# Two expert blocks as planned steps at the end of pass 1, and the weights of three relations made in a branch

## Chip, core and metric

The kernel runs on one core of one Trainium2 chip. TensorE (PE) multiplies matrices, VectorE (DVE), ScalarE (ACT) and GpSimd (POOL) work on rows, SyncE (SP) issues most transfers. All data begin and end in the chip's memory. The metric is the device time of one launch in microseconds: 2520.09, the median of three runs (2518.72 to 2521.66). The profile is one further execution, which took 2517.28 us; the span that its records cover is 2515.3 us.

## The reference

The input x is 64 x 256 rows (16,384 tokens) of 256 numbers, in fp32; adj is 64 x 256 x 256 integers, here 0 or 1. Two layers, each a graph step and a feed-forward step, all with a residual:

```python
x = x + gnn0(layernorm(x), adj)      # masked softmax attention over the neighbours
x = x + mamba2(layernorm(x))         # one chunk of 256, 8 heads, conv of 4, gate, RMS norm, W_out, W_lin
x = x + gnn1(layernorm(x), adj)      # sum over 4 relations r of (adj == r) @ x @ weight[r], + bias
x = x + moe(layernorm(x))            # below

logits = x @ gate_w + gate_b                          # 8 experts
idx, prb = argmax(softmax(logits)), max(softmax(logits))
pos = (rank of the token among those of its expert, in order of tokens)
kept = pos < 2560                                     # 1.25 * 16384 / 8
hmid = relu(buf[idx, pos] @ w1[idx] + b1[idx])        # 256 -> 1024
y = (hmid @ w2[idx] + b2[idx]) * prb * kept           # 1024 -> 256
x + nan_to_num(y, nan=0, posinf=1e4, neginf=-1e4)
```

Relation r counts the neighbours whose adj equals r, so with adj of 0 and 1 only the first relation contributes.

## The kernel before, in words

**Preparation** (L420 to L505). Weights are centred, so that the layer norms need no mean, and extended by columns that give the routing logits and row sums directly. Helpers work on one matrix at a time, with matmuls on TensorE and copies on VectorE, through a pool of two PSUM buffers: `centred` subtracts column means (L396), `projected` transposes a matrix, multiplies it by the gate weights and copies the result. The four relations' weights are loaded, centred and projected one after the other into `every`; the first is copied to `wrel` in on-chip memory, all four are stored to `wreld` in the chip's memory. Then follow the biases (L454), the attention vectors, W_out times W_lin, and b1, turned and stored (`b1d`).

**Pass 1** (L587 to L1163) takes 32 groups of two batch items, 512 tokens each, through both graph steps, the mamba step and the routing logits: `attention`, `scan`, `mix`, `relate`. `relate` makes hr = xhi, xlo times the adjacency (part of L585, where all products of the plan are recorded), multiplies it by `wrel`, adds the bias `brel` by an accumulating transfer into the tile x, adds the product (L1047), and issues two stores of x on SP, to `x3d` (a copy in the chip's memory from which pass 2 gathers) and to `out`. After each second group `choose` routes 1,024 tokens: some 25 small operations, a running count per expert (`seen`, L1103), two matmuls that turn counts into positions, and eight indirect scatters of (token, probability, row sum, row scale) into `slots`, an array of 2,560 places for each expert (L1123).

**The order of pass 1** is a plan. Every operation is a `Step` with an engine, an estimated duration and the tiles that it reads and writes; `Plan.record` builds all engines' streams by a list simulation. At each turn it takes, for each engine, the ready step that can begin earliest, and among those within 0.05 us the lowest rank, which is `PACE * g + DUE[k]` for step k of group g. Tiles are reused by tag, PSUM is eight banks given out by the simulation. Only these streams reach the chip, where engines wait for each other by semaphores; the simulated times do not.

**Between the passes.** `list_blocks` counts tokens per expert and makes the list of blocks for pass 2 on VectorE, in plain program order behind the plan. A test (`general`) sends adjacency values other than 0 and 1 to a branch (`again > 0`) that does pass 1 over with all four relations, read from `wreld`, through `AtOnce`, an executor that emits each step where it is written. With the inputs used here the branch is not taken.

**Pass 2** (L1195 to L1349) runs the experts over blocks of their places: wholes of 512 and halves of 256 rows, up to 40 and 8, each behind an `If` on the counts. A block loads its rows of `slots` (L1222) and its expert's w1, b1, w2, b2 (2 MB) on SP, gathers rows of `x3d` on POOL (L1251), scales them (L1260), transposes them (L1272), computes 8 hidden products with a relu on ScalarE (L1298, L1302) and, for each 128 rows, an output product of 8 matmuls (L1308), bias and scale (L1313, L1314), the guard against non-finite numbers, the residual (L1319 to L1328), and an indirect scatter to `out` (L1329). Loads and gathers of the next blocks are issued one or two blocks ahead; the first ones wait for pass 1's end.

Of the kernel before, what the change touches and what calls it, by code (L numbers as in the profile page):

```python
# [30 lines left out]
PACE = 21.50  # L31
DUE = [
    -273, -768, -7, 206, -128, -104, -233, 716, 257, 96, 325, 660, -290, -837, -1156, -195, -739,
    -864, 633, -563, -1270, 205, -488, -744, -1044, 252, -389, 419, -601, -43, 36, 132, 68, -155,
    389, 355, -223, -943, 4, 450, -281, 40, -502, 21, 982, 124, 113, 525, -49, 159, 104, 239, 309,
    -615, -359, -749, 426, 428, -391, -391, -326, -1237, -329, -546, -645, -815, -544, -187, -763,
    -683, -372, -601, -139, 290, -500, 172, -270, -586, 121, -388, 994, 458, -317, 125, 17, 277,
    17, 326, -210, -907, 100, -221, -383, -517, 6, 127, 610, 247, -329, -914, -875, -432, -1394,
    67, -309, 571, -93, -248, 110, 916, -78, 172, 34, 14, -122, 417, 67, 66, -569, 10, -1389, 19,
    -452, -183, -558, -20, 528, -605, -550, 387, -39, -686, -315, -111, -118, 33, 835, -632, -115,  # L40
    -192, 1375, -454, -252, 210, 224, 52, -419, -132, 69, 455, 629, 386, -646, 24, 58, 481, -861,
    -1548, -751, -773, 201, 9, 281, -95, 348, 383, 19, -696, -531, -135, -484, -660, 65, 182,
    -280, -194, -875, -1264, -1144, 84, 670, 265, 650, 324, 204, 363, 495, 947, 472, -54, 73, 119,
    -1092, -1060, -382, -668, -147, -96, -599, 715, 36, 69, -120, 106, -707, 33, 160, -559, 353,
    178, -313, 230, -326, -579, 295, 367, -2, -489, -468, -22, 96, -289, 98, -712, -377, 214, 73,
    287, -118, 62, -460, -77, -43, -515, 382, 530, -30, 249, 105, -328, 750, 213, -1302, -231,
    579, -503, -197, -40, 69, -338, -470, -134, -1067, -1028, -435, -550, -387, 677, -404, -211,
    -622, -957, -146, -304, 889, -297, 255, 165, 661, -161, -83, 166, -447, -657, -588, -282,
    -1432, -622, 134, -1056, -541, 582, -9, -25, 592, -45, 94, 540, 638, -1240, -75,
# [19 lines left out]
class AtOnce:  # L69
# [9 lines left out]

    def tile(self, tag, shape, dtype=F32, bufs=1):  # L80
        return Home(self.pool, tag, shape, dtype, self.KEPT.get(tag, 1))
# [12 lines left out]
class Step:  # L94
    def __init__(self, engine, us, go, g, tail, rank):
        self.engine, self.us, self.go, self.g = engine, us, go, g
        self.tail, self.rank = tail, rank
        self.waits, self.then, self.homes, self.ready = 0, [], [], 0.0


class Plan:
# [5 lines left out]
    HOP = 0.05  # L107

    def __init__(self, pool, banks):
        self.pool, self.banks = pool, banks  # L110
        self.steps, self.tags, self.known, self.g = [], {}, {}, 0

    def of(self, g, first=True):
        self.g, self.k = g, 0 if first else self.k
# [19 lines left out]
    def step(self, engine, us, go, reads, writes, late=0.0):  # L134
        step = Step(engine, us, go, self.g, self.TAIL[engine] + late, PACE * self.g + DUE[self.k])
        self.k += 1
# [38 lines left out]
    def record(self):  # L175
# [10 lines left out]
        left = len(self.steps)  # L186
        while left:
# [3 lines left out]
            for engine in range(5):  # L191
                found = None
                for step in ready[engine]:
                    t = max(step.ready, free[engine])
# [43 lines left out]
            for other in step.then:  # L238
                other.waits -= 1
                at = end + step.tail  # L240
                if step.engine != PE or other.engine != PE:
                    at += self.HOP
                other.ready = max(other.ready, at)
                if not other.waits:
                    ready[other.engine].append(other)
            undone[step.g] -= 1
# [7 lines left out]
def gnn_mamba_rgcn_moe(ctx: ExitStack, tc: tile.TileContext, a: dict, out: bass.AP):  # L254

# [42 lines left out]
    wreld = dram.tile([P, R, 2, D + E + 1], F32, name="wreld")  # L298
# [41 lines left out]
    work = const.tile([1, 2, 2, NBLK], I32, name="work")  # L340

# [46 lines left out]

    with tc.tile_pool(name="prep", bufs=1) as prep, tc.tile_pool(
        name="prep_ps", bufs=2, space=PSUM  # L390
    ) as prep_ps:
        def centred(dst, src, n):

            ps = prep_ps.tile([P, 512], F32, tag="ps", name="ps")
            for k in range(2):
                nc.tensor.matmul(  # L396
                    ps[:, :n], lhsT=ones_pp, rhs=src[:, k, :], start=(k == 0), stop=(k == 1)
                )
            for k in range(2):
                nc.vector.scalar_tensor_tensor(  # L400
                    dst[:, k, :], ps[:, :n], -1.0 / D, src[:, k, :], ALU.mult, ALU.add
                )

        def centre(w, n):
            for o in range(0, n, 512):
                centred(w[:, :, o : min(o + 512, n)], w[:, :, o : min(o + 512, n)], min(512, n - o))

        def projected(dst, src, n):

            for k in range(2):  # L410
                ps = prep_ps.tile([P, 512], F32, tag="ps", name="ps")
                for o in range(2):
                    nc.tensor.transpose(
                        ps[:, o * P : (o + 1) * P], src[:, k, o * P : (o + 1) * P], ident
                    )
                srcT = prep.tile([P, 2 * P], F32, tag="srcT", name="srcT", bufs=2)
                nc.vector.tensor_copy(srcT, ps[:, : 2 * P])
                ps = prep_ps.tile([P, 512], F32, tag="ps", name="ps")
                for o in range(2):
                    nc.tensor.matmul(  # L420
                        ps[:, :n], lhsT=srcT[:, o * P : (o + 1) * P], rhs=gq[:, o, :n],
                        start=(o == 0), stop=(o == 1),
                    )
                nc.vector.tensor_copy(dst[:, k, :], ps[:, :n])
# [9 lines left out]
        gq = wx[:, :, DA:WX]  # L434
        centred(gq, gq0, E + 1 + NH)
        nc.vector.memset(gq[:, :, E : E + 1], -1.0 / D)
        centred(wx[:, :, 0:D], w0, D)
        projected(wx[:, :, D:DQ], wx[:, :, 0:D], E + 1 + NH)
        centre(win, DPROJ - NH)
        every = prep.tile([P, R, 2, DG], F32, name="every")  # L440
        for r in range(R):
            nc.sync.dma_start(
                out=every[:, r, :, 0:D], in_=a["L1_gnn_weight"][r].rearrange("(k p) o -> p k o", p=P)
            )
            centre(every[:, r], D)
            projected(every[:, r, :, D:DG], every[:, r, :, 0:D], E + 1)
        nc.vector.tensor_copy(wrel[:, 0], every[:, 0])
        nc.sync.dma_start(out=wreld, in_=every)
        for vec, dst in (("L0_ffn_b_lin", blin), ("L1_gnn_bias", brel)):
            col = prep.tile([P, 2], F32, tag="col", name="col", bufs=2)  # L450
            nc.sync.dma_start(out=col, in_=a[vec].rearrange("(k p) -> p k", p=P))
            ps = prep_ps.tile([P, 512], F32, tag="ps", name="ps")
# [28 lines left out]
        projected(wl[:, :, D:DG], wl[:, :, 0:D], E + 1)  # L481
        woT = prep.tile([P, 2, DI], F32, name="woT")
        for k in range(2):
            ps = prep_ps.tile([P, DI], F32, tag="ps", name="ps")
# [5 lines left out]
        for c in range(NCT):  # L490
            ps = prep_ps.tile([P, DG], F32, tag="ps", name="ps")
# [9 lines left out]
        ps = prep_ps.tile([P, E * NFT], F32, tag="ps", name="ps")  # L501
# [36 lines left out]
    def list_blocks(pool, banks):  # L538


# [3 lines left out]
        ps = banks.tile([P, 512], F32, tag="ps1", name="ps")  # L544
        nc.tensor.matmul(ps[:, :E], lhsT=tri_b[:, 1, :], rhs=seen, start=True, stop=True)
        tot, nb, gap = (pool.tile([P, E], F32, name=n) for n in ("tot", "nb", "gap"))
        ends = pool.tile([P, 2, E], F32, name="ends")
        v.tensor_copy(tot, ps[:, :E])
        v.tensor_scalar(nb, tot, 256.0, None, ALU.is_gt)
        v.tensor_scalar(ends[:, 1, :], tot, 0.0, None, ALU.is_gt)  # L550
        for i in range(1, NB):
            v.scalar_tensor_tensor(nb, tot, 512.0 * i + 256.0, nb, ALU.is_gt, ALU.add)
            v.scalar_tensor_tensor(ends[:, 1, :], tot, 512.0 * i, ends[:, 1, :], ALU.is_gt, ALU.add)
        v.tensor_sub(ends[:, 1, :], ends[:, 1, :], nb)
        v.tensor_copy(ends[:, 0, :], nb)
        for e in range(1, E):
            v.tensor_add(ends[:, :, e : e + 1], ends[:, :, e : e + 1], ends[:, :, e - 1 : e])
        num_i = pool.tile([P, NBLK], I32, name="num_i")
        nc.gpsimd.iota(num_i, pattern=[[1, NBLK]], base=0, channel_multiplier=0)
        num = pool.tile([P, NBLK], F32, name="num")  # L560
        v.tensor_copy(num, num_i)
        for kind, n, limit in ((0, NBLK, NBLK), (1, E, 2 * NBLK)):
# [443 lines left out]
    def relate(s, js, o, full, xe, adjT, pair):  # L1006
# [42 lines left out]
        for view in (x3v, outv):  # L1049
            s.step(SP, 0.1, lambda view=view: nc.sync.dma_start(  # L1050
                out=view[:, js, :], in_=xe()[:, :, 0:D]), [xe], [], late=4.5)
# [332 lines left out]
```

## Time and profile before

| what | us |
|---|---|
| median of three runs | 2520.09 |
| the profiled execution | 2517.28 |
| its span | 2515.3 |
| TensorE busy | 2393.0 |
| VectorE busy | 1921.1 |
| ScalarE busy | 1641.2 |
| GpSimd busy | 838.2 |

The page divides the span into 40 slices of 62.9 us, and gives the busy tenths of each engine and the clock that was granted to TensorE. The trace can be cut into any stretches. In five of them TensorE was busy for:

| stretch (us) | what runs | length | TensorE busy | granted clock |
|---|---|---|---|---|
| 0 to 105 | preparation, first groups begin | 105 | 67.7 | 0.77 |
| 105 to 1600 | pass 1 | 1495 | 1484.6 | 1.00 |
| 1600 to 1800 | last four groups of pass 1 | 200 | 190.3 | 0.97 |
| 1800 to 1856 | last routing, list, first fetches | 56 | 6.3 | 0.54 |
| 1856 to 2504 | pass 2 | 648 | 644.1 | 0.99 |

A timeline row gives the time at which a group of equal instructions starts, its duration, engine, line, operation, destination and sources, shapes, how many instructions (x16), and in brackets the idle time of the engine before it and what ended it. A chain row gives start, duration, engine, tile and line.

### The profile page before, as it was taken

How to read it: one execution, taken by the hardware profiler on the slowest of the kernel's cores; microseconds unless marked ns; L12 is line 12 of the kernel's file. 1: busy time of each engine (PE TensorE's matmuls, PEld its weight loads, DVE VectorE, ACT ScalarE, POOL GpSimd, SP SyncE). 2: the span in 40 equal slices, each digit the busy share in tenths (PEclk: the TensorE clock that was granted, in tenths of full speed). 3: DMA queues.
4: the chain of work that ended last, by engine and by line, in shares of the span. 5: the costliest groups of instructions: out<-in, count | busy, mean ns of one | idle time of the engine just before them, and what ended most of it. 6: DMA issues, size and time to landing. Idle time of an engine off the chain costs nothing. (4 is left out here: it accounts for less than half of the span.)

```text
span 2515.3 us, 35051 instructions
## 1 busy us (share of the span) xinstructions
PE 2393.0 (95%) x11536; PEld 1667.4 (66%) x11536; DVE 1921.1 (76%) x4776; ACT 1641.2 (65%) x3712; POOL 838.2 (33%) x756
## 2 busy tenths in 40 slices
PE   6799999999999999999999999999559999999998
PEld 4566667766677776777766777666446666666665
DVE  3699999999999999999999999999623344334443
ACT  0688788888888888888888888888312222332232
POOL 0122343343333433334343343432532222222222
PEclk7899999999999999999999999999779999999999
DMA  2302222223222232222332222312264333333333
GB/s 79 100 12 64 63 54 62 64 67 75 54 62 54 71 79 56 54 62 70 68 67 53 62 68 57 81 37 54 52 194 122 122 107 116 120 115 117 110 124 74
DMA packets 171135, 196.53 MB, mean 78 GB/s; under 512 B 24919, under 2 KB 155807, under 8 KB 170800
## 3 DMA queue, kind: packets, MB, share of 16 engines
q1 hardware_dynamic: 122144, 133.11, 16.9%
q0 software_dynamic: 47104, 59.14, 12.7%
q8 instruction: 97, 1.59, 0.3%
q10 hardware_dynamic: 1680, 1.79, 0.2%
q14 instruction: 110, 0.90, 0.1%
HBM read 109.05 MB, written 47.06 MB: 62 GB/s over the span
## 5 line engine op out<-in xcount | busy, mean ns | idle before, releaser
L585 PE MATMUL ps<-xnT,win 128*128 128x512 f32 x1152 | 546.1, 600 | 3.9 <-ACT xnT L627 3.9
L804 DVE SCALAR_TENSOR_TENSOR y<-ps,cw,y 128x510 f32<-128x510 f32 (+2 forms) x480 | 349.6, 738 | 6.1 <-ACT y L797 2.8
L871 ACT ACTIVATE dm<-ps,cs 128x256 f32<-128x256 f32 (+1 forms) x1024 | 334.1, 475 | 11.5 <-PE ps L585 11.4
L593 POOL TENSOR_TENSOR rs<-ve,mhalf 128x4 f32<-128x4 f32 x96 | 155.1, 1616 | 508.2 <-DVE ve L591 490.3
L1298 PE MATMUL ps<-xnT,w 128*128 128x512 f32 (+1 forms) x768 | 318.0, 573 | 3.9 <-DVEq L1346 3.9
L1308 PE MATMUL ps<-w,hid 128*128 128x256 f32 x1440 | 318.7, 379 | 0.0
L585 PEld LDWEIGHTS ps<-xnT,win 128*128 128x128 f32 x1152 | 203.1, 190 | 166.1 <-issue 153.7
L1308 PEld LDWEIGHTS ps<-w,hid 128*128 128x128 f32 x1440 | 271.7, 190 | 44.9 <-issue 10.0
L1298 PEld LDWEIGHTS ps<-xnT,w 128*128 128x128 f32 x768 | 148.1, 193 | 161.2 <-issue 147.9
L585 PE MATMUL ps<-wf,gate 128*128 128x265 f32 x1024 | 251.9, 389 | 1.0 <-DVE gate L949 0.6
L1302 ACT ACTIVATE hid<-ps,b 128x512 f32<-128x512 f32 (+1 forms) x192 | 126.8, 661 | 183.1 <-PE ps L1298 183.1
L1313 DVE TENSOR_TENSOR yv<-ps,b 128x256 f32<-128x256 f32 x90 | 38.2, 425 | 254.4 <-PE ps L1308 254.4
L585 PEld LDWEIGHTS ps<-wf,gate 128*128 128x128 f32 x1024 | 192.8, 191 | 49.4 <-issue 11.3
L929 DVE TENSOR_TENSOR dm<-dm,bc 128x1536 f32<-128x1536 f32 x128 | 224.1, 1754 | 0.8 <-ACT dm L877 0.2
L1329 POOL DMA_INDIRECT out_dram<-yf,place x90 | 89.1, 990 | 372.3 <-DVE yf L1328 366.9
L877 ACT ACTIVATE dm<-dm 128x1536 f32<-128x1536 f32 x128 | 198.9, 1558 | 0.0
L1123 POOL DMA_INDIRECT slots<-meta,sl x128 | 133.5, 1043 | 191.0 <-DVE sl L1120 150.8
L1314 ACT ACTIVATE yv<-yv,meta 128x256 f32<-128x256 f32 x90 | 45.8, 508 | 201.5 <-DVE yv L1313 201.5
L936 PE MATMUL ps<-dm,xdt 128*64 128x256 f32 x1024 | 168.6, 396 | 4.7 <-DVE dm L929 4.4
L601 DVE BATCH_NORM_STATS2 st<-x 128x6 f32<-128x256 f32 x384 | 155.1, 416 | 6.1 <-DMA x<-in_x_dram 4.5
L954 POOL TENSOR_TENSOR xh<-xh 128x512 f32<-128x512 f32 x64 | 107.5, 1680 | 132.2 <-ACT xh L951 132.1
L585 PE MATMUL ps<-wh,eT 128*128 128x273 f32 x512 | 143.5, 405 | 0.0
(244 smaller groups left out, 4913.3 us busy)
## 6 DMA issues: line engine op xcount, KB each, us to landing
w<-in_L_ffn_w_dram SPq DMA_DIRECT2D x52, 1024.0 KB, 5.6
x<-blin POOLq DMA_DIRECT2D x32, 530.0 KB, 7.3
x<-brel POOLq DMA_DIRECT2D x32, 530.0 KB, 7.0
adji<-in_adj_dram SPq DMA_DIRECT2D x32, 512.0 KB, 3.9
x<-in_x_dram SPq DMA_DIRECT2D x32, 512.0 KB, 4.9
x3d<-x SPq DMA_DIRECT2D x32, 512.0 KB, 3.1
out_dram<-x SPq DMA_DIRECT2D x32, 512.0 KB, 4.1
cm<-bm SPq DMA_DIRECT2D x32, 128.0 KB, 2.2
```

What stands on the lines that cost most here:

```text
L585: nc.tensor.matmul(out_, lhsT=lhsT, rhs=rhs, start=(i == 0), stop=(i == len(pairs) - 1))
L593: s.step(POOL, 1.0, lambda: nc.gpsimd.tensor_tensor(rs(), ve(), mhalf[:, 0:4], ALU.pow), [ve], [rs])
L601: s.step(DVE, 0.34, lambda j=j: nc.vector.bn_stats(sb()[:, j, :], src()[:, j, 0:D]), [(src, j)], [(sb, j)])
L804: nc.vector.scalar_tensor_tensor(y3[:, :, d:], p3[:, :, : N - d], cw[:, c, k : k + 1], y3[:, :, d:], ALU.mult, ALU.add,)
L871: nc.scalar.activation(dm()[:, q, bi, o : o + n], ps()[:, t0 + N - n : t0 + N], AF.Relu, bias=cs()[:, j, h : h + 1], scale=-1.0,)
L877: s.step(ACT, 1.38, lambda: nc.scalar.activation(dm(), dm(), AF.Exp, scale=-1.0), [], [dm])
L929: s.step(DVE, 1.67, lambda dm=dm: nc.vector.tensor_mul(dm(), dm(), bc().unsqueeze(1).to_broadcast([P, 2, 2, N + P])), [bc], [dm])
L936: nc.tensor.matmul(o, lhsT=xdt()[:, 2 * bi, h * 64 : (h + 1) * 64], rhs=dm()[:, q, bi, 0:N], start=True, stop=False,)
L1123: s.step(POOL, 1.1, lambda j=j: apart("slots", nc.gpsimd.indirect_dma_start(out=slots, out_offset=bass.IndirectOffsetOnAxis(ap=sl()[:, j : ...
L1298: nc.tensor.matmul(ps[:, :n], lhsT=w1[:, k, f * P : (f + 1) * P], rhs=xnT[:, k, :], start=(k == 0), stop=(k == 1),)
L1302: nc.scalar.activation(hid[:, f, :], ps[:, :n], AF.Relu, bias=self.b1[i % 2][:, f : f + 1])
L1308: nc.tensor.matmul(ps[:, :D], lhsT=hid[:, f, j * P : (j + 1) * P], rhs=w2[:, f, :], start=(f == 0), stop=(f == NFT - 1),)
```

## The change

1. **First blocks early.** A list of two full blocks (`list_first`) is made once 28 of the 32 groups are routed, from `seen` as it stands then: an expert with n full blocks of 512 tokens gives up to n of the two, lowest experts first (`taken`). Two blocks (`NEARLY = 2`) then run as steps of the plan, with the operations of pass 2's wholes, in tiles that pass 1 has (`gate` and `xh` for w1 and w2, `x` or `dm` for hidden rows, `y` for results), in PSUM banks of the plan. They gather from the rows of `x3d` that 28 groups have stored, and scatter to `out` over what those groups stored there; a `rows_early` marker orders them behind these stores. `list_blocks`, as steps too, leaves the taken blocks out.
2. **Order.** Steps of blocks and lists have rank `PACE * 32 + LATE[k]`. Those on TensorE of over 0.4 us are held until at most `LEFT = 30` TensorE steps of the groups are left. `PACE` falls from 21.50 to 4.60, and all `DUE` have new values.
3. **Relations.** Preparation makes relation 1 alone, straight into `wrel`. The branch makes the other three with the same helpers. `wreld`, its store and its load go; `srcT` has one buffer where it had two.

Moves of code into helpers (`placed`, `gathered`, `normed`, `guarded`, `sent`) leave pass 2's own operations as they are.

```diff
-PACE = 21.50
+PACE = 4.60
 DUE = [
...
+LATE = [
...
 class Step:
+        self.held = late and engine == PE and us > 0.4
...
 class Plan:
+    LEFT = 30
+    def after(self, groups):
+        self.g, self.due = groups, "late"
...
+        due = (DUE if self.due == "group" else LATE)[k]
...
+        ahead = sum(step.engine == PE and not step.late for step in self.steps)
...
                 for step in ready[engine]:
+                    if step.held and ahead > self.LEFT:
+                        continue
...
+            ahead -= step.engine == PE and not step.late
...
+    def relation(pool, banks, dst, r):
+        nc.sync.dma_start(
+            out=dst[:, :, 0:D], in_=a["L1_gnn_weight"][r].rearrange("(k p) o -> p k o", p=P)
+        )
+        centred(pool, banks, dst[:, :, 0:D], dst[:, :, 0:D], D)
+        projected(pool, banks, dst[:, :, D:DG], dst[:, :, 0:D], E + 1)
...
-        for r in range(R):
-            nc.sync.dma_start(
-                out=every[:, r, :, 0:D], in_=a["L1_gnn_weight"][r].rearrange("(k p) o -> p k o", p=P)
-            )
-            centre(every[:, r], D)
-            projected(every[:, r, :, D:DG], every[:, r, :, 0:D], E + 1)
-        nc.vector.tensor_copy(wrel[:, 0], every[:, 0])
-        nc.sync.dma_start(out=wreld, in_=every)
+        relation(*own, wrel[:, 0], 0)
...
+    def list_first(s):
...
+        counted(s, tot)
...
+        def filled():
+            v.tensor_scalar(full(), tot(), 512.0, None, ALU.is_ge)
+            for i in range(2, NB + 1):
+                v.scalar_tensor_tensor(full(), tot(), 512.0 * i, full(), ALU.is_ge, ALU.add)
...
+    def first_block(s, b, stored, source):
+        w1, w2 = s.tile("gate", [P, NCT, 512], bufs=2), s.tile("xh", [P, NCT, 512], bufs=2)
...
+        s.step(SP, 3.5, fetch_slots, [listed_], [(side, "meta")], late=0.5)
+        s.step(SP, 9.0, fetch_weights, [listed_], [w1, w2, (side, "b")], late=2.0)
...
+        for j in range(4):
+            s.step(POOL, 1.1, lambda j=j: gathered(rows(xg, j), place()[:, 1, j : j + 1], source),
+                   [(side, "place"), stored], [(xg, j)], late=2.5)
...
+        for f in range(NFT):
+            s.step(PE, 1.72, lambda f=f, ps=ps: product(ps(), [
+                (flat(w1)[:, k * F + f * P : k * F + (f + 1) * P],
+                 flat(xnT)[:, k * 512 : (k + 1) * 512]) for k in range(2)]), [w1, xnT], [ps])
+            s.step(ACT, 0.58, lambda f=f, ps=ps: nc.scalar.activation(
+                hidden(f), ps(), AF.Relu, bias=b1()[:, f : f + 1]),
+                [ps, (side, "b")], [(hid[f // each], f % each)])
+        for j in range(4):
...
+            for f0 in range(0, NFT, 4):
...
+                s.step(PE, 1.73, summing, [w2, *hid], [ps])
...
     for g in range(NG):
         if g % 2 == 0:
-            pair = {}
+            pair = {"stored": [rows_early] if g < GEARLY else []}
         group(plan, g, slice(4 * g, 4 * g + 4), pair, tok[:, 4 * (g - 1) : 4 * (g + 1)])
+        if g == GEARLY - 1:
+            plan.after(NG)
+            list_first(plan)
+    plan.after(NG)
+    list_blocks(plan)
+    for b in range(NEARLY):
+        first_block(plan, b, rows_early, x3d[0 : GEARLY * 4 * P])
     with tc.manual_schedule(engines=ENGINES):
         plan.record()
-    list_blocks(pool, banks)
...
-        nc.sync.dma_start(out=every, in_=wreld)
+        nc.vector.tensor_copy(every[:, 0], wrel[:, 0])
+        for r in range(1, R):
+            relation(pool, banks, every[:, r], r)
```

Here `GEARLY` is 28, and `late=` in a step is planning data.

## The prediction

> **What bounds the kernel now.** I read the two digit rows of the page first. TensorE is busy nearly throughout; the only holes are the first slices, the slices just after 1760 us and the end. In those holes the granted clock falls as well.
>
> ```profile
> PE   6799999999999999999999999999559999999998
> PEclk7899999999999999999999999999779999999999
> ```
>
> The table by stretches puts numbers on it. From 200 to 1600 us TensorE idles about 1 us in 200 (199.0 busy, VectorE 190.6), so the body of pass 1 is TensorE's and has nothing to give. The hole between the passes is different:
>
> ```profile
> 1770.00:1780.00 10.00, 9.26 (x38) 7.07 (x39) 9.02 (x27) 1.52 (x3) 4.94 (x4) 0.66 0.01 2
> 1790.00:1800.00 10.00, 7.62 (x32) 6.28 (x31) 3.14 (x8) 5.10 (x15) 8.15 (x8) 0.83 0.70 131
> 1810.00:1830.00 20.00, 0.57 (x3) 0.21 (x2) 13.89 (x93) 0.12 (x1) 7.95 (x8) 0.50 0.03 5
> 1840.00:1856.00 16.00, 4.90 (x14) 2.50 (x15) 3.62 (x12) 1.62 (x4) 7.58 (x8) 0.50 1.04 337
> ```
>
> The first pair after the stretch is its length and TensorE's busy time; the last three numbers are granted clock, DMA share and GB/s. TensorE is all but empty from 1800.7 to 1855.2. The timeline tells what it waits for: the last group's outputs, their bias (an accumulating DMA), the routing, the list of blocks, then pass 2's first fetches.
>
> ```profile
> 1792.43 0.38 PE L585 MATMUL ps<-adjT,xhi 128*128 128x256 f32 x1 [2.10 <-ACT xhi L637]
> 1796.57 4.12 PE L585 MATMUL ps<-wrel,hr 128*128 128x265 f32 x16
> 1803.47 1.45 DVE L1047 TENSOR_TENSOR x<-ps,x 128x265 f32<-128x265 f32 x4 [7.35 <-DMA x<-brel]
> 1812.64 0.16 DVE L1103 TENSOR_TENSOR seen<-run,oh 128x8 bf16<-128x8 bf16 x1
> 1824.20 0.97 POOL L1123 DMA_INDIRECT slots<-meta,sl  x1 [0.30 <-issue]
> 1829.93 1.61 SPq L1222 DMA_DIRECT2D meta<-slots  x2
> 1855.18 8.91 PE L1298 MATMUL ps<-xnT,w 128*128 128x256 f32 x32
> ```
>
> Pass 2 then runs at TensorE's pace to the end. The chain of waits shows the period of a whole block, 1963.94 - 1935.52 = 28.42 us:
>
> ```profile
> 1935.52 13.73 PE ps L1298 x32
> 1949.25 6.91 PE ps L1308 x32
> 1957.03 6.91 PE ps L1308 x32
> 1963.94 13.73 PE ps L1298 x32
> ```
>
> How many blocks: L1302 ran 192 times, 8 per block, so 24; L1329 ran 90 times, 4 per whole and 2 per half. That makes 21 wholes and 3 halves.
>
> **Part 1, relations 2 to 4 leave the preparation.** Preparation is serial: TensorE and VectorE hand each relation back and forth, and pass 1 loads nothing until the last preparation tile is done (b1 stored at 65.88, first matmul on x at 73.87). The four starts:
>
> ```profile
> 31.58 2.05 PE L396 MATMUL ps<-every,tri 128*128 128x256 f32 x4
> 38.29 2.05 PE L396 MATMUL ps<-every,tri 128*128 128x256 f32 x4
> 45.01 2.05 PE L396 MATMUL ps<-every,tri 128*128 128x256 f32 x4
> 51.72 1.86 PE L454 MATMUL ps<-wx,col 128*128 128x9 f32 x8
> ```
>
> 51.72 - 31.58 = **20.1 us** goes, for three relations. What is late next would be W_lin's load, needed at about 33.5 in the new order; it was issued at 15.1 and took 9.0, so it is there at 24, and three loads of 1.75 us of issue time go from ahead of it. The store of all four (1,060 KB, issued at 52.10) and a 0.44 us copy lay beside other work: nothing. srcT now has one buffer; TensorE's own order already held the second transpose behind the first product, so nothing. The branch itself is not taken.
>
> **Part 2, pass 2 loses two wholes.** After 28 groups 14,336 tokens are counted over 8 experts, so one expert has at least 1,792, three full blocks: two are always found. Pass 2 keeps 19 wholes: 2 x 28.42 = **56.8 us** go from it.
>
> **Part 3, the same work in the hole.** In the built order the blocks' transposes stand behind the last group's head products, two hidden products ahead of its relation step, and the rest behind. By the rows they need 8 x 1.72 + 16 x 0.864 + 1.0 = 28.4 us each, again 56.8. Filled by them: the idle times 0.66 + 2.11 + 0.28 in the stretch 1774 to 1800.7 (3.05 us), and slow matmuls. Here a rule is to be weighed. The Trainium skill, "TensorE: Matmul & The Clock Gate", section "Why this matters for your kernels", lets the clock fall only after idle gaps above some 3 us; by it nothing but 3.05 us is gained. The row shows gaps of 1.10 and 1.76 us (at 1766.9 and 1769.0) followed by a granted clock of 0.66 and 24 output products in 7.25 us where the same 24 took 5.65 at 1756.8; after the 2.11 us gap the last group's products come at 0.21 us where the group before had 0.12 (12 x 0.097 = 1.2), and wrel takes 4.12 for 3.79. The row decides: 3.05 + 1.5 = 4.5 us.
>
> The new waits. (a) The routing products of the last pair stand on TensorE behind 12.05 us of block work (5 + 1 hidden products, one quarter sum: 6 x 1.72 + 1.73) after wrel; before, they were ready 12.1 us after it (1812.64 to 1812.8 against 1800.7). What is queued behind them is the rest of both blocks, 38 us. Any lateness of the chain is thus a TensorE stall. Late it may be: four sums of squares on ScalarE share it with relus of 0.66, and the second block's 2 MB of weights, issued when the last group's output products free their buffers (about 1785), meet the bias accumulate issued at 1795.44. The skill's "DMA: Bandwidth & Descriptors", section "Issuing engines are not separate DMA queues", speaks against the change: all transfers interleave on the same 16 engines whoever issued them. By it 2.1 MB at the trace's best 337 GB/s delay the bias by 6.2 us, all of it a stall; by the row a weight load lands 5.6 us after issue, so both are over before the bias starts: 0. I take 3, nearer to the row in part, since two loads follow each other. (b) VectorE gets the first list (some 45 small operations at about 0.12 us from the list's own row of 1812.9 to 1825.2: 5.5 us), 8 norms of 0.41 and 4 casts: 9.5 us in groups 30 and 31, where it is busy 9.0 to 9.9 of 10 us until 1780. Hidden entirely: 0. Wholly on the path: 9.5. I take 3, as it has 3 us in 10 to do from 1790 on. POOL's eight gathers (1.28 us apart) and SP's 12 fetches find idle queues; SP's x stores of groups 30 and 31 stand behind weight fetches whose buffers are free by then: 0, at worst within (a).
>
> So TensorE ends the blocks at 1800.7 - 4.5 + 56.8 + 3 + 3 = 1859.0 on the old clock. The list (12.3 us of VectorE) and the slot scatters run beside it.
>
> (c) Pass 2's first fetch still waits for every engine and every DMA of pass 1, so the last block's finish is exposed. From the end of the page's run: last product ends 2503.97, last scatter issues 2507.62: 3.65. Two row blocks now end 1.73 us apart, so one more round on VectorE, 3.0; landing 3.3 (median of that scatter); landing to fetch 3.1 (slots scatter 1824.20 + 2.6 to 1829.93). 13.0 us, fetch at 1872.0 instead of 1829.9: 42.1 later. From the fetch to the first product, 25.3 us, nothing changes: TensorE is cold both times.
>
> **Sum.** 20.1 + 56.8 - 42.1 = 34.8 us. The profiled execution took 2517.3 (span 2515.3), so 2482.5 there; the median of the runs shown is 2520.1, 2.8 above it: **2485 us**.
>
> The changed planner constants: up to about 137 us the built order of TensorE is the same, so the ramp is; later each pair of groups has some five steps in another place, with the same instructions. Idle there is 1 us in 200, so at most some 8 us can be gained; a loss is bounded below.
>
> **Rivals.** *Blocks wait for the routing* (0.20): the chain of (a) is 20 us late, from contention and ScalarE. The stall is 20 instead of 3; the hole then gives -2 and only part 1 stays: 2502. For it: VectorE already waited 7.35 us for that bias; against: the bias needs no more bytes than before. *All hidden* (0.11): (a) and (b) cost nothing and the two last row blocks finish as one with their landing half covered: 12 less, 2473. For it: the order leaves TensorE 12 us of cover; against: VectorE's row. *The body slows down* (0.07, the slower side): one mechanism, VectorE. It has 4.5% of slack in 200 to 1600 us, and in each pair of groups steps now stand elsewhere in its queue; if a late dm or y product holds TensorE in every pair (101 us, from x stores first at 235.2 and last at 1805.4, 31 intervals of 50.65), 15 pairs at 2.3 us undo the 35. At 3 us each: 2530. Against it: the same instruction counts and much the same order. That fewer than two blocks are taken is excluded above.
>
> **Numbers.** Forecast 0.60, its own range 2474 to 2496; the remaining 0.02 lies within 0.2% (5 us, about what a measurement here can tell from no change). Faster 0.91, same 0.02, slower 0.07. The range takes in the bounds of (a) and (b), 2469 to 2504.
>
> **What will show it.** The first matmul on x near 54 us; 19 wholes of 28.4; TensorE busy from 1780 to about 1839 on the new clock, with at most 6 us idle before the routing products; the first slots fetch of pass 2 some 13 us after the last early product. It is wrong if TensorE idles long behind the routing products, if the body's 50.65 us per group changes by over 0.2, or if the fetch comes before the blocks are done.

## The result: 35 us on one chip, nothing on another

On the chip of the first comparison the changed kernel took 2485.25 us (2484.87 to 2487.95, four runs) against 2520.41 before: ratio 0.9863, interval 0.9846 to 0.9880. The forecast was 2485. The profiled execution took 2487.95 us with a span of 2486.2.

The experiments ran on three chips, and there the same program did otherwise. I call the chip of the first comparison A, the others B, C and D. Which chip A was is not on record; it may be B, where before takes 2520.1 too. Each of B, C and D served for one short time only, so a chip and its moment can't be told apart here.

| chip | before | after | ratio (interval) |
|---|---|---|---|
| A | 2520.4 | 2485.3 | 0.9863 (0.9846 to 0.9880) |
| C | 2557.7 | 2545.0 | 0.9957 (0.9942 to 0.9971) |
| D | 2524.0 | 2526.4 | 1.0008 (0.9999 to 1.0017) |

So the forecast is right for A. On D the gain is gone, as in the sum of the slower rival (2.3 us in each of 15 pairs of groups). On C before itself takes 37 us more than on A. First A, by its own trace. The digit rows of the page after (TensorE, then its granted clock): the hole is narrower and the clock no longer falls to 7.

```profile
PE   5899999999999999999999999999967999999997
PEclk8999999999999999999999999999988999999999
```

Preparation, in the timeline: relation 1 at 24.55, straight on to the bias columns at 29.35, first product on x at 51.95 instead of 73.87.

```profile
24.55 1.13 PE L438 MATMUL ps<-wrel,tri 128*128 128x256 f32 x4 [0.94 <-DVE win L442]
29.35 1.85 PE L498 MATMUL ps<-wx,col 128*128 128x9 f32 x8
51.95 1.94 PE L734 MATMUL ps<-ident,x 128*128 128x128 f32 x8 [9.94 <-DMA x<-in_x_dram]
```

The end of pass 1 on all engines, in order of time: the last group's wrel step, the blocks' hidden products behind it, the routing (VectorE at 1803.17, TensorE at 1803.81 with no wait in brackets), the last quarter sums, the last scatter on GpSimd, the first fetch on SP, and pass 2.

```profile
1788.15 3.79 PE L697 MATMUL ps<-wrel,hr 128*128 128x265 f32 x16
1791.78 8.74 PE L697 MATMUL ps<-xnT,gate 128*128 128x512 f32 x20
1803.17 0.16 DVE L1215 TENSOR_TENSOR seen<-run,oh 128x8 bf16<-128x8 bf16 x1
1803.81 0.19 PE L697 MATMUL ps<-oh,tri_b 128*128 128x64 bf16 x1
1829.02 13.65 PE L1376 MATMUL ps<-xh,dm 128*128 128x256 f32 x62 [0.23 <-ACT dm L1367]
1848.72 0.97 POOL L1271 DMA_INDIRECT out_dram<-y,hide  x1 [1.43 <-DVE y L1390]
1853.27 1.23 SPq L1496 DMA_DIRECT2D meta<-slots  x2
1864.04 0.66 PE L1539 MATMUL ps<-ident,xn 128*128 128x128 f32 x2 [21.37 <-DMA b<-in_L_ffn_b_dram]
1877.51 9.42 PE L1565 MATMUL ps<-xnT,w 128*128 128x256 f32 x32
```

The stretch table says it in two rows (length, TensorE busy): full to 1840, then almost empty for as long as exposed finish and fetch take.

```profile
1800.00:1840.00 40.00, 39.77 (x156) 28.70 (x155) 30.46 (x148) 9.29 (x16) 12.73 (x13) 1.00 0.06 18
1840.00:1880.00 40.00, 9.24 (x31) 5.81 (x30) 8.67 (x30) 3.14 (x7) 14.46 (x15) 0.60 0.65 209
```

Pass 2 has 19 wholes and 3 halves (L1569 ran 176 times, L1271 82 times for them), at the old period, 1987.47 - 1959.05 = 28.42 in the chain:

```profile
1959.05 13.73 PE ps L1565 x32
...
1987.47 13.73 PE ps L1565 x32
```

### The profile page after: what moved, and what is told of

Its sections match the earlier page's. It is cut to its first block, busy times and chain, and to the rows that moved or that the text cites. A ratio compares the mean times of both kernels' runs of the same rounds, so it can differ in the third digit from the quotient of the medians.

```text
span 2486.2 us, 34990 instructions
## 1 busy us (share of the span) xinstructions
PE 2378.8 (96%) x11489; PEld 1660.2 (67%) x11489; DVE 1918.6 (77%) x4811; ACT 1639.7 (66%) x3712; POOL 828.7 (33%) x756
## 3 DMA queue, kind: packets, MB, share of 16 engines
q1 hardware_dynamic: 121184, 131.24, 16.5%
## 5 line engine op out<-in xcount | busy, mean ns | idle before, releaser
L705 POOL TENSOR_TENSOR rs<-ve,mhalf 128x4 f32<-128x4 f32 x96 | 161.2, 1679 | 523.2 <-DVE ve L703 399.4
L1565 PE MATMUL ps<-xnT,w 128*128 128x512 f32 (+1 forms) x704 | 290.6, 572 | 4.7 <-DVE xn L1259 4.7
L1575 PE MATMUL ps<-w,hid 128*128 128x256 f32 x1312 | 290.4, 379 | 0.0
L1575 PEld LDWEIGHTS ps<-w,hid 128*128 128x128 f32 x1312 | 247.6, 190 | 40.9 <-issue 9.1
L1565 PEld LDWEIGHTS ps<-xnT,w 128*128 128x128 f32 x704 | 136.3, 194 | 147.6 <-issue 135.0
L1569 ACT ACTIVATE hid<-ps,b 128x512 f32<-128x512 f32 (+1 forms) x176 | 115.8, 658 | 168.5 <-PE ps L1565 168.5
L697 PEld LDWEIGHTS ps<-wf,gate 128*128 128x128 f32 x1024 | 191.8, 190 | 48.0 <-issue 11.2
L1580 DVE TENSOR_TENSOR yv<-ps,b 128x256 f32<-128x256 f32 x82 | 34.8, 425 | 243.0 <-PE ps L1575 243.0
L1271 POOL DMA_INDIRECT out_dram<-yf,place x82 | 81.2, 990 | 349.5 <-DVE yf L1588 344.0
L1235 POOL DMA_INDIRECT slots<-meta,sl x128 | 127.9, 1000 | 195.2 <-DVE sl L1232 149.1
L922 ACT ACTIVATE xh<-y 128x512 f32<-128x512 f32 x160 | 101.0, 632 | 75.3 <-DVE y L916 65.9
```

Source lines behind the costliest of these rows:

```text
L697: nc.tensor.matmul(out_, lhsT=lhsT, rhs=rhs, start=(i == 0), stop=(i == len(pairs) - 1))
L705: s.step(POOL, 1.0, lambda: nc.gpsimd.tensor_tensor(rs(), ve(), mhalf[:, 0:4], ALU.pow), [ve], [rs])
L1235: s.step(POOL, 1.1, lambda j=j: apart("slots", nc.gpsimd.indirect_dma_start(out=slots, out_offset=bass.IndirectOffsetOnAxis(ap=sl()[:, j : ...
L1565: nc.tensor.matmul(ps[:, :n], lhsT=w1[:, k, f * P : (f + 1) * P], rhs=xnT[:, k, :], start=(k == 0), stop=(k == 1),)
L1569: nc.scalar.activation(hid[:, f, :], ps[:, :n], AF.Relu, bias=self.b1[i % 2][:, f : f + 1])
L1575: nc.tensor.matmul(ps[:, :D], lhsT=hid[:, f, j * P : (j + 1) * P], rhs=w2[:, f, :], start=(f == 0), stop=(f == NFT - 1),)
```

## Where the 35 us came from on chip A, step by step

Each row is a stretch between the same events in the two traces, after minus before, in us:

| stretch | predicted | measured | miss |
|---|---|---|---|
| to the first product on xnT (103.48, 82.24) | -20.1 | -21.2 | -1.1 |
| from there to TensorE's last product ahead of pass 2, blocks included (1800.69, 1842.67) | +58.3 | +63.2 | +4.9 |
| from there to the first fetch (1829.93, 1853.27) | -16.2 | -18.6 | -2.4 |
| fetch to first hidden product (1855.18, 1877.51) | 0 | -1.0 | -1.0 |
| halves (wholes start at 1903.80, 1927.49) | 0 | +1.4 | +1.4 |
| wholes to the last product (2503.97, 2470.65) | -56.8 | -57.0 | -0.2 |
| last product to the end of the span | 0 | +4.2 | +4.2 |
| sum | -34.8 | -29.1 | +5.7 |

The two profiled spans thus differ by 29.1, not 35. The rest lies in the executions: the profiled one of before was 3.1 us below the median of 2520.41, that of after 2.7 above its own. To that extent the exact hit is luck.

The stretch of 63.2 is 6.4 more than the two blocks' 56.8; the prediction had allowed 1.5 more (6 of stalls, less 4.5 of filling), and so missed 4.9. The 6.4 have three parts. The body is one, 1.7: from group 4 to group 30 (counted from 0) the lead over before (how much earlier a group's first product on eT starts) falls from 23.5 to 19.5, after a gain of 2.3 in the first groups. The waits of TensorE from 600 to 1600 us show why; before, and then after (waiting for whom: us, times, longest):

```profile
PE ps L585 <- ACT xnT L627: 2.3, 10, 0.2
PE ps L622 <- ACT xn L637: 2.1, 10, 0.2
```

```profile
PE ps L697 <- ACT eT L835: 3.7, 10, 0.4
PE ps L697 <- ACT xnT L739: 2.1, 9, 0.2
PE ps L734 <- ACT xn L749: 1.9, 9, 0.2
```

One line is new: in each pair of groups TensorE now stands 0.37 us before a product on eT, whose copy by ScalarE has ended only 0.05 us earlier. The second part is idle time from 1700 us to the last product, 9.7 us against 8.1. What is left, some 3 us, is slower products: the clock stood at half for four stretches of 3.4 us in the last groups, against 10.2 us in all before. How much of the 3 us that makes was not measured apart.

## Experiments

**Part 1 alone (chip B): confirmed.** Preparation and branch of after, all else as before.

```diff
-        for r in range(R):
...
-            projected(every[:, r, :, D:DG], every[:, r, :, 0:D], E + 1)
+        relation(*own, wrel[:, 0], 0)
```

> Kernel before with part 1 alone (relations 2 to 4 made only in the branch). The prediction's sum: 20.1 us faster than before, 2500. From the two traces, where the first product on xnT starts 21.2 us earlier: 2499, and the lead stays flat through pass 1. Rival (the first loads of x bound the start anyway): under 12 us faster, 2508 or more.

2499.14 against 2520.10 (ratio 0.9918, 0.9904 to 0.9931): 21.0 us. The lead in the trace is 21.2 to 21.3 in every group from 3 to 30. The rival falls: x is waited for 9.9 us where it was 8.5, so the first load takes back 1.5 us and not 10.

**The new order alone (chip B): it costs 10.6 us.** `PACE` and `DUE` of after in the kernel before.

```diff
-PACE = 21.50
+PACE = 4.60
```

> Kernel before with the new PACE and DUE alone. The prediction: body unchanged, 2520 within 2 us. Theory from the traces (the lead falls by 0.15 us per group from group 4 to 30, about 4 us, after a gain of about 2 in the first four groups): 2 to 4 us slower, 2522 to 2525, with 0.3 us more per pair of groups in the trace. Rival: the loss belongs to the early blocks' steps in the same plan, then this is 0 to 2 us faster.

2530.65 against 2520.10 (1.0042, 1.0029 to 1.0056). All three expectations were too low. The body does what the trace of after showed, with the same line, so the loss is the order's and not the blocks':

```profile
PE ps L586 <- ACT eT L724: 3.6, 10, 0.4
```

It adds 1.9 us by group 30. Another 9.0 are lost in the last two groups: without blocks to put between, TensorE waits there for relation inputs (5.2 us for xhi, 3.8 for xlo). The hole after it is 2.8 shorter, and the rest of the span 4.4 longer, nearly all of it at its close (last section). The new order needs blocks at the end.

**Both parts in the old order (chips B and D).**

```diff
-PACE = 4.60
+PACE = 21.50
```

> Kernel after with PACE and DUE of before, late steps kept in the same place against group 31. Theory from the traces (new order costs 0.15 us per group): the lead over before stays flat from group 4 to 30 and the time is 2 to 4 us below after, 2481 to 2483. The prediction (order costs nothing): 2485. Rival (the new order earns its place at the end, where blocks and groups mix): slower than after, 2487 or more.

> Kernel after with PACE and DUE of before throughout, now beside after. Theory from the waits (new order: 0.37 us per pair for the copy of eT; at the end both orders reach the first fetch within 1.4 us of each other): 0 to 3 us below after where before takes 2520, 10 to 20 us below where it takes 2557. Rival (the medians of the first two calls, 2489 against 2485): 3 to 4 us above after.

On B 2488.96 against 2520.10 (0.9879, 0.9864 to 0.9894), on D 2491.84 against 2523.96 (0.9876, 0.9861 to 0.9891). It takes 31 to 32 us off on either chip. After did not run on B. The profiled spans, 2485.4 here and 2486.2 for after on A, show no gain from the new order; the medians, 2489.0 and 2485.3, lean the other way, and neither decides between runs that may be of two chips. On D it is 34.5 us faster than after.

**One block instead of two (chip B).**

```diff
-    NEARLY = 2
+    NEARLY = 1
```

> Kernel after with one early block instead of two. Pass 2 gets one whole back, 28.4 us. The prediction's sum has each block cost its 28.4 in the hole as long as TensorE is what ends last there: 2485. Theory from the trace (with one block the list and the slots scatters end last, at about 1824 on the clock of after, so the fetch comes at about 1827 instead of 1853): the second block is worth only 2 us, 2487. Rival (both blocks worth the same, half of the gain in the hole): about 7 us slower than after, 2492.

2495.44 (0.9904, 0.9889 to 0.9919). Theory and prediction both fall, and the rival comes nearest: by the traces (last products at 2476.5 and 2470.7, on B and A) the second block is worth 5.8 us, and the medians, from the same two places, differ by 10.2. What ends last is neither TensorE nor the slots but the one block's finish: its output sums end at 1810.5, but VectorE works at the list until 1817.0 and finishes the four row blocks after it. TensorE shows this as one wait:

```profile
1824.11 0.59 PE L1437 MATMUL ps<-others,tri 128*128 128x1 f32 x2 [13.66 <-DVE y L1382]
```

The fetch comes at 1831.83, not at 1827. With two blocks, the same VectorE work lies beside the second one's products.

**After again (chips C and D): the gain goes in the body.**

> The kernel after, unchanged, beside the three runs below. 2485.25 as before, 2484 to 2488 by the scatter of its four runs; its profiled execution was 2487.95. Theory: its GpSimd closing drain is again 6.2 us long (2.1 in the kernel before), since every program with the new order or the blocks showed it.

> The kernel after, beside the others of this call. On a chip where before takes 2520: 2485. Where before takes 2557: about 2545 as in the last call, since the new order of the body leaves TensorE more often behind the late VectorE product than the old one.

> The kernel before, unchanged, for its trace beside those below: ratio 1. On a chip where its time is 2520, TensorE waits in the body twice per pair of groups for 0.2 us. If its time is near 2557 as in the last call, the theory is that VectorE stands still for about 2 us once per pair with its semaphores fulfilled (as in the trace of after there), so that the body, not the end, holds the 37 us.

Before, again on D, is 0.9998 (0.9989 to 1.0007) of itself. After is 1.0008 on D. Every step at the two ends is there as on A: lead 20.8 us at the first eT product, fetch 10.6 us after the last early product on D, 10.8 on C. Between, the lead over before on A turns from 22.3 at group 5 into a lag of 16.5 at group 29 on D, 1.6 us per group, and on C from 24.2 ahead to 30.4 behind, 2.3 per group. TensorE's waits from 600 to 1600 us on D, after and then before:

```profile
PE ps L1048 <- DVE dm L1041: 22.4, 9, 2.5
PE ps L697 <- ACT eT L835: 3.4, 9, 0.4
```

```profile
PE ps L585 <- ACT xnT L627: 2.3, 10, 0.2
PE ps L622 <- ACT xn L637: 2.1, 10, 0.2
PE ps L936 <- DVE dm L929: 1.1, 2, 0.6
```

A late dm holds TensorE 2.5 us in nearly every pair. That is the wait which the slower rival named, at about its price. The view of the tile xdt tells why dm is late: this product of VectorE lies ahead of it. After on D:

```profile
L1031 DVE TENSOR_TENSOR xdt<-ps,dt x112: 654/685/693, 200.2 to 1676.2; 128x512 f32<-128x512 f32 x112
its engine sat idle before it (us, times) until:
  PE ps L697: 30.2, 26
```

The durations are those of A (651/677/692 ns); what is new is that VectorE sits idle before it, where on A the view lists no idle time at all. The same place on A, then on D with TensorE and ScalarE:

```profile
311.11 1.89 DVE L1031 TENSOR_TENSOR xdt<-ps,dt 128x512 f32<-128x512 f32 x3
```

```profile
311.78 1.47 PE L1026 MATMUL ps<-ident,xh 128*128 128x128 f32 x12
313.31 0.69 DVE L1031 TENSOR_TENSOR xdt<-ps,dt 128x512 f32<-128x512 f32 x1 [0.64 <-PE ps L1026]
315.46 0.69 DVE L1031 TENSOR_TENSOR xdt<-ps,dt 128x512 f32<-128x512 f32 x1 [1.46 <-PE ps L697]
317.00 1.36 ACT L983 ACTIVATE dm<-ps,cs 128x256 f32<-128x256 f32 x4 [1.26 <-PE ps L697]
```

The transposes that these xdt read were over at 313.25. But VectorE does not see that; it waits for a semaphore that TensorE raises when a product is done, and the trace has records of its raising. On A the record follows the product's end by about 0.014 us, and the waiting instruction starts some 0.025 us later. On D nothing is recorded from 313.29 to 315.44, though products that raise this semaphore ended at 313.91 and 314.13; 23 ns after the record of 315.44 the xdt starts. All 30 gaps of over 0.3 us before xdt on D end like this, 22 to 24 ns after a record. ScalarE waits in the same way: 13 times beside the scatters of `choose` on D, 16.6 us in all, where on A it does so once, for 0.5 us.

The next table counts, from 200 to 1700 us, the gaps of over 0.3 us before xdt, and then the instructions of TensorE, VectorE and ScalarE that raise a semaphore with no record within 0.15 us of their end (late or missing). Both are sorted by whether GpSimd was issuing the eight scatters of `choose` (from the first issue to 2 us after the last):

| program, chip | xdt gaps beside the scatters | xdt gaps elsewhere | late records beside the scatters | late records elsewhere |
|---|---|---|---|---|
| before, A | 0 of 52 | 0 of 60 | 3 of 684 | 0 of 5813 |
| after, A | 0 of 56 | 0 of 58 | 0 of 759 | 0 of 5872 |
| after, D | 30 of 52, 33.6 us | 0 of 60 | 291 of 614 | 0 of 5849 |
| after, C | 34 of 42, 44.2 us | 0 of 67 | 258 of 588 | 0 of 5800 |
| before, D | 0 of 52 | 0 of 60 | 272 of 680 | 0 of 5802 |
| both parts in the old order, D | 3 of 56, 3.3 us | 0 of 60 | 286 of 724 | 0 of 5771 |
| old order to group 27, C (below) | 0 of 48 | 0 of 62 | 264 of 643 | 1 of 5692 |

So on C and D the semaphores of three engines are raised late while the scatters are issued, in either order of instructions, and nearly never on A. The two orders differ in what comes to wait for them. On D the old one falls behind its own time on A by only 2.5 us up to group 30; in the new one xdt waits, with dm and TensorE behind it. Both orders put xdt beside the scatters, and on A with the same slack (a median of 0.37 us from the end of its transposes to its start), so why it is caught in the new one alone stays open. The Trainium skill, "SBUF — State Buffer", section "Who interferes with whom", has VectorE and GpSimd share one pair of memory ports, but says that a VectorE operation with at most one operand in that memory (xdt's other one is in PSUM), outside the modes that use two port pairs, does not contend with GpSimd. The rows give no reason to doubt it: xdt lasts about as long on D as on A (medians of 685 and 677 ns), its gaps end with TensorE's semaphore, and ScalarE waits for that one too. This also answers the theory that VectorE stands still "with its semaphores fulfilled". Open, too, is why the semaphores are late beside the scatters, and only in the runs on C and D. Moving the scatters elsewhere was not tried.

**Old order up to group 27, new at the end (chip C).**

```diff
+        rank = PACE * self.g + due + 473.0
+        if self.due == "group" and self.g < 28:
+            rank = 21.50 * self.g + BODY[k]
```

> Kernel after with the order of before for groups 0 to 27, and the new one for groups 28 to 31 and the late steps. Theory (the new order loses 0.15 us per group in the body, by a wait of 0.37 us per pair of TensorE for the copy of eT, and earns its place only at the end): lead flat at 22.2 us, then the end of after: 2 to 3 us below after. Rival (the two orders don't join well at group 28, or the end needs the body's order): same as after or slower.

2526.54 against 2557.73 for before and 2545.02 for after there (0.9878, 0.9860 to 0.9897). The size was wrong, since chip C was not expected; the direction holds, 18.5 us. The old order isn't immune on C: its lead over before on A turns from 22.6 at group 5 into a lag of 11.4 at group 27. Its stall sits one operation later (before `bc`, 11 of 12 times beside the scatters, 21.4 us in all, none elsewhere).

**Blocks held until the groups are done (chip C): they cover the routing.**

```diff
-    LEFT = 30
+    LEFT = 0
```

> Kernel after with LEFT 0 instead of 30: no large TensorE step of the early blocks ahead of the groups' last step. The prediction's term (early products fill 4.5 us of idle time in the last groups): 4 to 5 us slower than after. Theory from the traces (TensorE's idle time from 1700 us to the end of the blocks is no smaller than before, 9.6 against 8.1 us, so the three hidden products put ahead filled nothing net): within 1.5 us of after.

2565.30 (1.0035, 1.0024 to 1.0046), 20.3 above after there; the profiled executions differ by 14.7. Both expectations fall. TensorE in the timeline, after the last wrel step:

```profile
1841.63 4.41 PE L697 MATMUL ps<-wrel,hr 128*128 128x265 f32 x16
1854.61 0.21 PE L697 MATMUL ps<-oh,tri_b 128*128 128x64 bf16 x1 [8.56 <-DVE oh L1207]
1855.98 0.21 PE L697 MATMUL ps<-run,tri_b 128*128 128x64 bf16 x1 [1.16 <-DVE run L1213]
```

With nothing to put between, the routing stalls TensorE for 9.7 us, and the last relation step waits 5.9 us for xlo where after waits 2.6. That is the rival "blocks wait for the routing", brought about by holding the blocks; in after the 12 us of block work ahead of the routing products hide it wholly. My expectation had forgotten this cover, which the prediction had counted.

**The first whole's transposes behind the halves (chip C): the other half of the hole.**

```diff
-            self.turned(self.norm(0), 0)
+        def turn_first(self):
+            self.turned(self.norm(0), 0)
...
         blocks.begin()
+        if blocks is halves:
+            blocks.turn_first()
     for blocks in (halves, wholes):
+        if blocks is wholes:
+            blocks.turn_first()
```

> Kernel after with the transposes of pass 2's first whole block moved from ahead of the halves to behind them. Theory (from the first fetch to the first hidden product 24.2 us pass, of which TensorE waits from 1866.6 to 1877.5 only for the gathers of that whole, since its transposes stand ahead of the first half's products): first hidden product about 10 us earlier, 3 us given back at the change from halves to wholes: 7 us below after. Rival (the weights and biases of the first half, all landed only at about 1864, bound it as well): under 3 us.

2536.59 (0.9922, 0.9904 to 0.9940), 8.4 below after there, as expected. From fetch (1911.47) to first hidden product 13.6 us pass instead of 25.0:

```profile
1924.03 0.69 PE L1539 MATMUL ps<-ident,xn 128*128 128x128 f32 x2 [0.97 <-DVE xn L1259]
1925.09 9.24 PE L1567 MATMUL ps<-xnT,w 128*128 128x256 f32 x32 [0.37 <-ACT xnT L1542]
```

The last product is 8.1 us earlier, so 3 are given back at the change to wholes.

**Both together (chip D): faster than either kernel.**

> The order of before for groups 0 to 27, the new one at the end, and the transposes of the first whole behind the halves. If the two gains add (2 to 3 and 7 to 8 us on a chip where before takes 2520; 18 and 8 where it takes 2557): 2475 or 2519, the fastest of all.

2487.14 against 2523.96 before and 2526.38 after (0.9858, 0.9843 to 0.9873). It meets neither 2475 nor 2519. Against the old order throughout it gains 4.7 us there, less than the sum of the two. By the traces the transposes are worth 5.9 us (11.1 less 5.2 given back), and the new end nothing: TensorE's last product ahead of pass 2 comes 1.6 us earlier, and 1.4 of that was there from the first group on.

## Why the prediction was right, and where it wasn't

- **Part 1** is right in mechanism and size (20.1; 21.0 measured alone). **Part 2** is all but exact (56.8; 57.0).
- **Filling the hole by 4.5** was wrong in sign against before: idle time at the end went from 8.1 to 9.7. The blocks do fill holes, but such as the new order itself opens. On C, from group 31's first product on eT to the end of its relation step, 110.6 us pass in after with 8.6 us of block work among them, and 112.4 with the blocks held, so they fill some 10 us.
- **Stall (a), 3,** was 0: the routing was ready 0.5 us before its turn. The weights' transfers did not delay it. **(b), 3,** is inside the idle time above.
- **(c), 13.0,** was 10.6. The last scatter followed the last product by 6.05 (6.65 in the sum), and the first fetch followed that scatter by 4.55 (6.4 in the sum).
- **Missing:** GpSimd's closing drain (last section), 4.2, and the body's 4.0.
- **Slips in the sum:** 8 x 1.72 + 16 x 0.864 + 1.0 is 28.6, not 28.4, for a block. The rows name 3.1 us of slow products in the hole (1.6, 1.2 and 0.3), of which the 4.5 takes 1.5 without a reason. The range of 2474 to 2496 does not take in 2469 to 2504, as it says.
- **"Idle there is 1 us in 200, so at most some 8 us can be gained; a loss is bounded below"** is the step that failed away from A. It counted what TensorE has to give, and left what TensorE can be made to wait to a rival. That rival, with 0.07, named the right wait (a late dm in every pair) at about the right price, but held VectorE's little slack to be the reason; what made dm late were semaphores that were raised late. The prediction's own sign, the body's 50.65 us per group changing by over 0.2, came up: 0.15 on A, 1.6 on D, 2.3 on C. On the two other chips where after ran, it takes some 22 us of the gain (C) or all of it (D). The moved order deserved a part and a price of its own, and a test alone: without blocks it loses 10.6 us even on B.

## What to carry to other kernels

A hole is filled by moving work only as far as what stays behind it allows: here the first block covers the routing, and the second VectorE's work on the list. Change an instruction order and the work separately, since a good part of one can hide the loss of the other. And a body with no idle time on the bound engine has no cover either: a delay of 2 us to another engine passes through in full where the order has the bound engine wait for it. The old order lost little to the same late semaphores on D, so an order is to be timed on more than one chip or occasion.

## What the hardware showed unasked

- **The closing drain of GpSimd**, an instruction of the kernel's last line, took 2.1 us in before and with part 1 alone, and 6.2 (6.0 to 6.3) in every program with the new order or with blocks, on all chips. The view of the kernel's last line on GpSimd, before and after (minimum/median/maximum in ns):

```profile
L1380 POOLq DRAIN  x3: 50/111/2117, 2512.3 to 2515.0; - x3
```

```profile
L1636 POOLq DRAIN  x3: 50/111/6242, 2479.1 to 2485.9; - x3
```

It ends about 11.2 us after the last scatter's issue instead of 6.8. The order alone brings it about; why is open.
- **The clock can fall after short gaps.** In after, TensorE's gap of 2.0 us at 1739.5 is followed by 3.4 us at half clock (last three numbers: granted clock, DMA share, GB/s), and so were gaps of 1.2 and 1.6 us. It need not: before's gap of 2.2 us at 1721.3 was not, and on D, of thirteen gaps of 2.2 to 2.5 us in the body, three were.

```profile
1742.17:1745.58 3.41, 3.19 (x12) 2.60 (x12) 3.40 (x7) 3.41 (x11) 0.20 (x1) 0.50 0.13 38
```
